# A quad's sums over states in another order, and the steps around a selective scan moved by one tick

## The chip, the core and the metric

The kernel runs on one core of a Trainium2 chip. Five instruction streams work side by side: TensorE (PE in the profile; its weight loads are PEld), VectorE (DVE), ScalarE (ACT), GpSimd (POOL) and SyncE (SP), which here issues nearly all DMAs. Each stream takes its instructions in the order in which the program holds them, and they meet through semaphores. The metric is the device time of one run in microseconds (us): 1186.88 us is the median of three runs of the kernel before (1186.69 to 1189.98).

## The reference

The input is x, 4 sequences of 1024 tokens with 256 features, all in float32. One layer is computed, in two parts:

```
h   = layernorm(x);  u = rmsnorm(h) * norm1_w
z, xs, B, C, dt_raw = split(u @ in_proj_w.T)        # 256, 64, 64, 256, 128 columns
dt  = softplus(dt_raw @ dt_proj_w.T + b)
state = exp(dt * A) * state + (dt * xs) * B          # per channel and state, along 1024 tokens
y   = (sum over states of state * C + xs * D) * silu(z)
h   = h + y @ out_proj_w.T
x   = x + h + (silu(n @ gate.T) * (n @ up.T)) @ down.T    # n = rmsnorm(h) * norm2_w, width 704
x   = x + (fwht(silu(v @ W1.T) * (v @ W3.T))) @ W2.T      # v = layernorm(x), width 1024
```

There are 256 channels with 32 states each: 8192 recurrences for each sequence. The Walsh-Hadamard transform (fwht) is worked into W2 once, at the start.

## The kernel before

**Units and quads.** The tokens are cut into eight units of 512 (two for each sequence, `us`). The recurrences of a unit are cut into 16 quads (`qs`, 128 in all); a quad holds four tiles (b = 0 to 3) of 128 partitions (32 states x 4 channels) by 512 tokens. The second unit of each sequence (units 1, 3, 5, 7, called odd here) starts its states from the `carry` of the first; the even ones start from a constant.

**Ticks.** The order of all instructions is written out by hand, by a loop over ticks at the end of `tile_block`. A quad takes two ticks, a half of it (two tiles) each; a unit takes 32 ticks. In tick T, for the quad q = T // 2, the loop emits, stream by stream:

- PE: the steps of lane `PE`, then (in even ticks) `sum_states(q - 1)`, then lane `PEend`
- ACT: lane `ACT`, then `copy_b` where there is one, two `exp` for the quad after this one (they are what the scans of tick T + 2 read), then lane `ACTend`
- DVE: `times_b` for the two tiles, a scan, the steps of lane `DVE`, the other scan
- POOL: lane `POOL0`, `times_c` for the two tiles scanned in tick T - 1, `start_from` (odd units: the first column of the tiles of tick T + 1 times the carry), then lane `POOL`
- SP: DMA issues: `ub` for tick T + 6, `da` for three quads on, `cr` for two quads on

The four steps of a tile are `da = exp(dt * A)` (ACT, L725), `bx = ub * B` (DVE, L749, two tiles in one), the scan (DVE, L759) and the product with C (POOL, L777, two tiles in one). `sum_states` (L791) then sums over states with four matmuls against a 0/1 matrix, one for each tile, into four groups of 32 output partitions. Each of these float32 matmuls appears twice in the profile. A `da` tile has four buffers, and one is loaded again when the sums have read it. B stands in PSUM as `pb`, one buffer, copied by `copy_b` (L738) every 16 ticks, between the last `times_b` that reads the old one and the first that reads the new one.

**The steps around the scan.** `pre(u, H)` prepares unit u, whose first tick is H, during the ticks of the unit before: normalization (`un`, transposed to `ut`), the projections of x, B and dt (`pe_x`), dt (`pe_dt`), C (`pe_c`) and z (`pe_z`). `post(u, E, other)` does what follows the scan of unit u, whose last tick is E, during the ticks of the next unit, here with ticks counted from E:

- E+3: out_proj, 8 matmuls on PE (`add_rows` with `wo`, L306); two DVE adds at E+4 (L316)
- E+5 to E+9: row statistics, 1/sqrt (`small2`, POOL), scaling (`hn`, ACT), transposes to `ht`
- E+10 and E+13: `gated` on `m`, three chunks each: gate and up projections (PE, L226), `silus` and the copies `up` (ACT, L263 and L270), products (POOL, L274); the z of the unit after next rides along as a further projection
- E+18: down projection (`add_rows` with `wd`), statistics, `hn`, transposes to `xt` at E+25
- E+26, E+29, E+32: `gated` on `g` in chunks of 3, 3 and 2; E+36: `add_rows` with `w2h`; E+43: store

So E+32 is tick E of the next unit: while out_proj of unit u runs, the last chunk of `g` of the unit before and then its `w2h` matmuls run too. The steps of `pre` for the unit after next fall in the same ticks: with H = E + 33, H-30 is E+3, H-25 is E+8, H-16 is E+17.

The lines that matter in `gated`, for a group that starts at `tick`:

```
for k, step in enumerate(steps):
    at(tick + k // 2, "PE", *step)          # gate projections, z, up projections
at(tick + 1, "ACTend" if three else "ACT", silus)
at(tick + 2, "ACT", up, 0)                  # the others: ACTend of tick + 2
at(tick + 2, "POOL", product, 0)            # the others: tick + 3
```

PSUM has four buffers for all dense results (`ps_m`); `ht`, `xt`, `ut` and `yt` share three buffers, `un` and `hn` share one.

Of the kernel before, what the change touches and what calls it, by code (L numbers as in the profile page):

```python
# [11 lines left out]
ALU = mybir.AluOpType  # L12
# [8 lines left out]
TT = T // P  # L21
# [6 lines left out]
def tile_block(ctx: ExitStack, tc: tile.TileContext, a, out):  # L28
# [20 lines left out]
    nc = tc.nc  # L49
# [15 lines left out]
    def dense_psum():  # L65
        return ps_m.tile([P, T], F32, tag="dense", name="dense")
# [141 lines left out]
    def transposes(u, src):  # L208

        u["pt"] = [dense_psum() for _ in range(2)]  # L210
        for k in range(2):
            for t in range(TT):
                nc.tensor.transpose(  # L213
                    u["pt"][k][:, t * P : (t + 1) * P], src[:, t, k * P : (k + 1) * P], ident
                )
# [22 lines left out]
    def at(tick, lane, fn, *args):  # L238
        todo[tick][lane].append(partial(fn, *args))
# [5 lines left out]
    def gated(tick, u, dst, wa, wb, chunks, src, z=None):  # L245


        g = [{} for _ in chunks]
        pe_z, act_z = z[0]["z"] if z else (None, None)

        def pe(i, name, w):
            c, n = chunks[i]
            if n < P:

                both = project(W[w], c * P, 2 * n, u[src])
                g[i]["pg"], g[i]["pu"] = both, both[n:]
            else:
                g[i][name] = project(W[w], c * P, n, u[src])

        def silus():  # L260
            for i, (_, n) in enumerate(chunks):
                g[i]["si"] = p3.tile([P, T], F32, tag="si", name="si")
                nc.scalar.activation(g[i]["si"][:n], g[i]["pg"][:n], AF.Silu)  # L263
            if z:
                act_z(z[1])

        def up(i):
            n = chunks[i][1]
            g[i]["up"] = p3.tile([P, T], F32, tag="up", name="up")
            nc.scalar.copy(g[i]["up"][:n], g[i]["pu"][:n])  # L270

        def product(i):
            c, n = chunks[i]
            nc.gpsimd.tensor_tensor(u[dst][:n, c, :], g[i]["si"][:n], g[i]["up"][:n], ALU.mult)  # L274

        three = len(chunks) == 3
        steps = [(i, *s) for s in (("pg", wa), ("pu", wb)) for i in range(len(chunks))]
        steps = [s for s in steps if chunks[s[0]][1] == P or s[1] == "pg"]
        late = z and len(steps) == 6
        steps = [(pe, *s) for s in steps]  # L280
        if z:
            steps.insert(3, (pe_z, z[1]))
        for k, step in enumerate(steps):
            at(tick + k // 2, "PE", *step)
        at(tick + 1, "ACTend" if three else "ACT", silus)
        at(tick + 2, "ACT", up, 0)
        for i in range(1, len(chunks)):
            if i == 2 and late:
                at(tick + 3, "ACT", up, i)
            else:  # L290
                at(tick + 2, "ACTend", up, i)
        at(tick + 2, "POOL", product, 0)
        for i in range(1, len(chunks)):
            at(tick + 3, "POOL", product, i)
# [29 lines left out]
    def pre(u, H):  # L324

        s = {}
# [217 lines left out]
        if H == 32:  # L544

            at(0, "ACTend", lambda: row_stats(u, u["x"], (0, 1)))
            at(1, "ACTend", lambda: row_stats(u, u["x"], (2, 3)))
            at(3, "POOL", small)
            at(5, "POOL", small_end)
            at(4, "ACT", un, (0, 1))  # L550
            at(5, "ACT", un, (2, 3))
            at(6, "PE", lambda: transposes(u, s["un"]))
            at(6, "ACTend", transposed, u, "ut")
        else:
            at(H - 54, "SP", load_x, u)
            at(H - 45, "ACTend", lambda: row_stats(u, u["x"], (0, 1)))
            at(H - 43, "ACTend", lambda: row_stats(u, u["x"], (2, 3)))
            at(H - 39, "POOL", small)
            at(H - 37, "POOL", small_end)
            at(H - 32, "ACT", un, (0, 1))  # L560
            at(H - 31, "ACT", un, (2, 3))
            at(H - 30, "PE", lambda: transposes(u, s["un"]))
            at(H - 30, "ACTend", transposed, u, "ut")
        at(H - 25, "PE", pe_x)
        at(H - 24, "ACT", act_x)
        at(H - 23, "SP", dma_xb)
        at(H - 19, "SPend", dma_xr, 0)
        at(H - 17, "SPend", dma_xr, 1)
        at(H - 16, "PE", pe_dt)
        at(H - 16, "PE", pe_c, 0)  # L570
        if H == 32:
            for h in range(2):
                at(H - 11, "PE", pe_z, h)
# [16 lines left out]
    def post(u, E, other):  # L590


        s = {}
# [41 lines left out]
            4,  # L635
            "PEend",
        )
        at(E + 5, "ACTend", lambda: row_stats(u, u["hr"], (0, 1), False))
        at(E + 6, "ACTend", lambda: row_stats(u, u["hr"], (2, 3), False))
        at(E + 7, "POOL", small2)  # L640
        at(E + 8, "ACT", hn, "r3", None)
        at(E + 9, "PE", lambda: transposes(u, s["tok"]))
        at(E + 9, "ACTend", transposed, u, "ht")
        at(E + 9, "POOL", lambda: nc.gpsimd.tensor_tensor(u["hr"], u["hr"], u["x"], ALU.add))
        at(E + 10, "PE", big, "m")
        sizes = [min(P, DFF - c * P) for c in range(6)]
        chunks = list(enumerate(sizes))
        for i in range(2):
            gated(E + 10 + 3 * i, u, "m", "wg", "wu", chunks[3 * i : 3 * i + 3], "ht",
                  (other, i) if other else None)  # L650
        add_rows(
            E + 18,
            u,
            lambda: [u["m"][:n, c, :] for c, n in enumerate(sizes)],
            lambda: [W["wd"][:n, c, :] for c, n in enumerate(sizes)],
            1,
        )
        at(E + 20, "ACTend", lambda: row_stats(u, u["hr"], (0, 1)))
        at(E + 22, "ACTend", lambda: row_stats(u, u["hr"], (2, 3)))
        at(E + 23, "POOL", small3)  # L660
        at(E + 24, "ACT", hn, "r4", "nm")
        at(E + 25, "PE", lambda: transposes(u, s["tok"]))
        at(E + 25, "ACTend", transposed, u, "xt")
        at(E + 26, "PE", big, "g")
        chunks8 = [(c, P) for c in range(8)]
        for i in range(3):
            gated(E + 26 + 3 * i, u, "g", "w1", "w3", chunks8[3 * i : 3 * i + 3], "xt")
        add_rows(
            E + 36,
            u,  # L670
# [113 lines left out]
    def sum_states(q):  # L784
        s = qs[q]
        u = s["u"]
        first, last = s["n"] % 8 == 0, s["n"] % 8 == 7
        if first:
            u["py"] = ps_y.tile([P, T], F32, tag="y", name="py")
        for b in range(4):  # L790
            nc.tensor.matmul(  # L791
                u["py"][32 * b : 32 * b + 32, :],
                lhsT=rsel[:, 2 * s["j"] + s["g"], :],
                rhs=s["da"][:, b, :],
                start=first,
                stop=last,
            )
        if last:
            at(2 * q + 3, "DVE", y_dx, u, s["h"])
            at(2 * q + 4, "POOL0", y_z, u, s["h"])  # L800
# [13 lines left out]
    for k, u in enumerate(us):  # L814
        pre(u, 32 * k)
# [37 lines left out]
    tick = min(todo)  # L853
# [106 lines left out]
```

## Time and profile before

| what | value |
|---|---|
| time, median of 3 runs | 1186.88 us (1186.69 to 1189.98) |
| the profiled execution's own time | 1190.86 us |
| its span (first to last instruction) | 1189.1 us |
| mean granted TensorE clock | 0.903 |
| DVE busy | 961.1 us (81%) |
| PE busy | 1023.6 us (86%) |
| POOL busy | 903.0 us (76%) |
| ACT busy | 773.8 us (65%) |
| first scan starts, last scan ends | 22.2 us, 1074.0 us |

How to read it: groups of instructions are named by line, engine and operation, output <- inputs; then how often, busy us and mean ns of one, and, behind the second bar, the idle time of the engine right before them and what ended it. A wait is "engine, line of what waited <- engine, line of what it waited for: us in total, times, longest". A row of the timeline is start us, us, engine, line, operation, output <- inputs, number of merged instructions; in square brackets is the idle time before it with its releaser. A row of windows is a stretch (from:to, length) and then the busy us of PE, PEld, DVE, ACT and POOL, each with its number of instructions, the granted PE clock, the busy share of the DMA engines and GB/s. The rows of one period quoted later are of unit 3 (fourth of eight), where E is tick 95 and tick 96 begins its scans at 419.17 us.

### The profile page before, as it was taken

The numbers are of one execution on the slowest core, as the hardware profiler recorded it, in microseconds if no ns is written. First come the engines' busy times: TensorE is split into PE (matmuls) and PEld (weight loads), VectorE is DVE, ScalarE is ACT, GpSimd is POOL, SyncE is SP. The second block draws the span as 40 slices with busy tenths as digits, with TensorE's granted clock in tenths as the row PEclk, the third lists the DMA queues.
The fourth block names the chain that finished last, engine by engine and source line by source line (L and its number), as shares of the span: only waits on it lengthen the run. The fifth ranks groups of instructions, "written<-read, shape, count | busy, mean of one in ns | idle before, by whom it ended". The sixth has DMA issues, their size and how long they took to land.

```text
span 1189.1 us, 12244 instructions
## 1 busy us (share of the span) xinstructions
PE 1023.6 (86%) x3374; PEld 471.1 (40%) x3374; DVE 961.1 (81%) x860; ACT 773.8 (65%) x1391; POOL 903.0 (76%) x807
## 2 busy tenths in 40 slices
PE   8475467989998989988998989988998989699988
PEld 3121022433633355433634354433634353336535
DVE  4797889899889979899889979898989989992000
ACT  3746564878478775879478767878576847573331
POOL 6675768879788978889788978889787978784212
PEclk9776668989898889989998989988998989889989
DMA  7989998898699879888799869998689869840000
GB/s 246 336 308 355 358 338 296 310 329 284 238 337 306 327 244 313 318 327 296 252 339 313 302 225 342 313 335 282 242 315 322 308 243 328 307 155 1 18 0 18
DMA packets 89444, 321.91 MB, mean 271 GB/s; under 512 B 9312, under 2 KB 20000, under 8 KB 73120
## 3 DMA queue, kind: packets, MB, share of 16 engines
q1 hardware_dynamic: 87520, 318.38, 75.7%
q10 hardware_dynamic: 1856, 2.75, 0.6%
q8 instruction: 27, 0.44, 0.1%
q14 instruction: 41, 0.34, 0.1%
HBM read 302.22 MB, written 18.87 MB: 270 GB/s over the span
## 4 chain that ended last, share of the span: by engine, by line
PE 44%; POOL 16%; DVE 10%; issue 8%; DMA 4%; ACT 4%; SPq 0%; DVEq 0%; POOLq 0%; ACTq 0%
PE dense L226 23%; PE dense L306 14%; POOL da L777 10%; PE py L791 6%; DVE da L759 5%; DVE bx L749 4%; POOL g L274 3%; ACT da L725 1%; DMA ub<-ud 1%; DMA cd<-cc 1%; POOL m L274 1%; DVE hr L316 1%; PE dense L213 1%; DMA xr<-xbd 1%; POOL yt L811 1%
## 5 line engine op out<-in xcount | busy, mean ns | idle before, releaser
L777 POOL TENSOR_TENSOR da<-da,cr 128x1024 f32<-128x1024 f32 x256 | 603.7, 2358 | 100.1 <-DVE da L759 52.2
L759 DVE TENSOR_TENSOR_SCAN da<-da,bx 128x512 f32<-128x512 f32 x512 | 602.0, 1210 | 43.7 <-ACT da L725 10.4
L725 ACT ACTIVATE da<-da,nega 128x512 f32<-128x512 f32 x508 | 331.4, 713 | 68.8 <-DMA da<-dtd 65.4
L791 PE MATMUL py<-da,rsel 128*32 128x512 f32 x1024 | 226.7, 685 | 134.7 <-POOL da L777 132.8
L749 DVE TENSOR_TENSOR bx<-ub,pb 128x1024 f32<-128x1024 f32 x254 | 312.1, 1229 | 30.5 <-ACT pb L738 19.2
L226 PE MATMUL dense<-xt,w 128*128 128x512 f32 x512 | 228.8, 601 | 0.0
L226 PEld LDWEIGHTS dense<-xt,w 128*128 128x128 f32 x512 | 95.6, 191 | 136.0 <-issue 111.8
L791 PEld LDWEIGHTS py<-da,rsel 128*32 128x32 f32 x1024 | 29.9, 113 | 270.7 <-POOL da L777 213.8
L316 DVE TENSOR_TENSOR hr<-hr,dense 128x512 f32<-128x512 f32 x48 | 32.4, 675 | 127.6 <-PE dense L306 127.6
L306 PE MATMUL dense<-w2h,g 128*128 128x256 f32 x512 | 113.4, 380 | 0.0
L306 PE MATMUL dense<-wd,m 128*128 128x256 f32 (+1 forms) x384 | 103.6, 417 | 0.9 <-POOL m L274 0.9
L306 PEld LDWEIGHTS dense<-w2h,g 128*128 128x128 f32 x512 | 96.8, 190 | 18.4 <-issue 5.5
L270 ACT COPY up<-dense 128x512 f32<-128x512 f32 x112 | 63.4, 578 | 58.3 <-PE dense L226 58.1
L274 POOL TENSOR_TENSOR g<-si,up 128x512 f32<-128x512 f32 x64 | 80.8, 1272 | 25.8 <-ACT up L270 25.4
L226 PE MATMUL dense<-ut,win 128*128 128x512 f32 x192 | 94.1, 623 | 0.2 <-ACT ut L220 0.2
L274 POOL TENSOR_TENSOR m<-si,up 128x512 f32<-128x512 f32 (+1 forms) x48 | 60.4, 1273 | 41.3 <-ACT up L270 41.3
L226 PE MATMUL dense<-ht,wg 128*128 128x512 f32 x192 | 89.4, 610 | 2.6 <-ACT ht L220 2.6
L263 ACT ACTIVATE si<-dense 128x512 f32<-128x512 f32 x112 | 63.0, 596 | 39.7 <-PE dense L226 38.1
L306 PEld LDWEIGHTS dense<-wd,m 128*128 128x128 f32 (+1 forms) x384 | 72.3, 201 | 40.0 <-issue 24.0
L200 ACT ACTIVATE hn<-hr,s 128x256 f32<-128x256 f32 x64 | 30.3, 543 | 88.9 <-POOL s L196 74.8
L226 PE MATMUL dense<-ht,wu 128*128 128x512 f32 x160 | 72.2, 597 | 0.0
L776 POOL COPY carry<-da 128x2 f32<-128x2 f32 x128 | 23.8, 186 | 61.5 <-DVE da L759 59.5
(92 smaller groups left out, 798.5 us busy)
## 6 DMA issues: line engine op xcount, KB each, us to landing
da<-dtd SPq DMA_DIRECT2D x127, 1024.0 KB
ub<-ud SPq DMA_DIRECT2D x254, 512.0 KB
cr<-cd SPq DMA_DIRECT2D x64, 256.0 KB
x<-in_x SPq DMA_DIRECT2D x8, 512.0 KB
dtd<-dt SPq DMA_DIRECT2D x16, 256.0 KB
ud<-du SPq DMA_DIRECT2D x16, 256.0 KB
cd<-cc SPq DMA_DIRECT2D x16, 256.0 KB
out<-hr SPq DMA_DIRECT2D x8, 512.0 KB
```

The source lines that it names most:

```text
L200: nc.scalar.activation(dst[:, t, :], src[:, t, :], AF.Identity, bias=bias[:, t : t + 1] if bias is not None else 0.0, scale=scale[:, t : t ...
L226: nc.tensor.matmul(dst[:n], lhsT=w[:, k, col : col + n], rhs=src[:, k, :], start=(k == 0), stop=(k == 1),)
L263: nc.scalar.activation(g[i]["si"][:n], g[i]["pg"][:n], AF.Silu)
L270: nc.scalar.copy(g[i]["up"][:n], g[i]["pu"][:n])
L274: nc.gpsimd.tensor_tensor(u[dst][:n, c, :], g[i]["si"][:n], g[i]["up"][:n], ALU.mult)
L306: nc.tensor.matmul(po[t // 2][:, t % 2, :], lhsT=left[k][:, t * P : (t + 1) * P], rhs=right[k], start=(k == 0), stop=(k == n - 1),)
L316: nc.vector.tensor_tensor(hr, hr, po[i], ALU.add)
L725: nc.scalar.activation(da, da if q else s["u"]["pdt", b], AF.Exp, scale=an[:, s["h"], s["j"], b, s["g"] : s["g"] + 1],)
L749: nc.vector.tensor_tensor(s["bx"], s["ub", b0 // 2], u["pb"].unsqueeze(1).broadcast_to([P, 2, T]), ALU.mult)
L759: nc.vector.tensor_tensor_scan(da, da, s["bx"][:, b % 2, :], start, ALU.mult, ALU.add)
L777: nc.gpsimd.tensor_tensor(s["da"][:, two, :], s["da"][:, two, :], s["cr"].unsqueeze(1).broadcast_to([P, 2, T]), ALU.mult,)
L791: nc.tensor.matmul(u["py"][32 * b : 32 * b + 32, :], lhsT=rsel[:, 2 * s["j"] + s["g"], :], rhs=s["da"][:, b, :], start=first, stop=last,)
```

## The change

`sum_states` multiplies the tiles in the order 2, 3, 0, 1 instead of 0, 1, 2, 3. Nearly all steps of `post` from the row statistics after out_proj to the last gated group are emitted one tick earlier, as are `un`, its transposes, `pe_dt` and the first `pe_c` of `pre`; both halves of the first row statistics stand in one tick. out_proj itself, its adds, `pe_x`, `act_dt`, `copy_b`, and the `w2h` matmuls keep their ticks. `silus` of the group of two chunks goes to the end of its tick on ACT. The first unit's and the second unit's preparation keep most of their ticks.

```diff
-        three = len(chunks) == 3
...
-        at(tick + 1, "ACTend" if three else "ACT", silus)
+        at(tick + 1, "ACTend", silus)
...
-            at(H - 32, "ACT", un, (0, 1))
-            at(H - 31, "ACT", un, (2, 3))
-            at(H - 30, "PE", lambda: transposes(u, s["un"]))
-            at(H - 30, "ACTend", transposed, u, "ut")
-        at(H - 25, "PE", pe_x)
-        at(H - 24, "ACT", act_x)
-        at(H - 23, "SP", dma_xb)
+            at(H - 33, "ACT", un, (0, 1))
+            at(H - 32, "ACT", un, (2, 3))
+            at(H - 31, "PE", lambda: transposes(u, s["un"]))
+            at(H - 31, "ACTend", transposed, u, "ut")
+        x = max(H - 25, 7)
+        at(x, "PE", pe_x)
+        at(x + 1, "ACT", act_x)
+        at(x + 2, "SP", dma_xb)
...
-        at(H - 16, "PE", pe_dt)
-        at(H - 16, "PE", pe_c, 0)
+        at(H - 17, "PE", pe_dt)
+        at(H - 17, "PE", pe_c, 0)
...
-        at(E + 5, "ACTend", lambda: row_stats(u, u["hr"], (0, 1), False))
-        at(E + 6, "ACTend", lambda: row_stats(u, u["hr"], (2, 3), False))
-        at(E + 7, "POOL", small2)
-        at(E + 8, "ACT", hn, "r3", None)
-        at(E + 9, "PE", lambda: transposes(u, s["tok"]))
-        at(E + 9, "ACTend", transposed, u, "ht")
-        at(E + 9, "POOL", lambda: nc.gpsimd.tensor_tensor(u["hr"], u["hr"], u["x"], ALU.add))
-        at(E + 10, "PE", big, "m")
+        at(E + 5, "ACTend", lambda: row_stats(u, u["hr"], range(TT), False))
+        at(E + 6, "POOL", small2)
+        at(E + 7, "ACT", hn, "r3", None)
+        at(E + 8, "PE", lambda: transposes(u, s["tok"]))
+        at(E + 8, "ACTend", transposed, u, "ht")
+        at(E + 8, "POOL", lambda: nc.gpsimd.tensor_tensor(u["hr"], u["hr"], u["x"], ALU.add))
+        at(E + 9, "PE", big, "m")
...
-            gated(E + 10 + 3 * i, u, "m", "wg", "wu", chunks[3 * i : 3 * i + 3], "ht",
+            gated(E + 9 + 3 * i, u, "m", "wg", "wu", chunks[3 * i : 3 * i + 3], "ht",
...
         add_rows(
-            E + 18,
+            E + 17,
...
-        at(E + 20, "ACTend", lambda: row_stats(u, u["hr"], (0, 1)))
-        at(E + 22, "ACTend", lambda: row_stats(u, u["hr"], (2, 3)))
-        at(E + 23, "POOL", small3)
-        at(E + 24, "ACT", hn, "r4", "nm")
-        at(E + 25, "PE", lambda: transposes(u, s["tok"]))
-        at(E + 25, "ACTend", transposed, u, "xt")
-        at(E + 26, "PE", big, "g")
+        at(E + 19, "ACTend", lambda: row_stats(u, u["hr"], (0, 1)))
+        at(E + 21, "ACTend", lambda: row_stats(u, u["hr"], (2, 3)))
+        at(E + 22, "POOL", small3)
+        at(E + 23, "ACT", hn, "r4", "nm")
+        at(E + 24, "PE", lambda: transposes(u, s["tok"]))
+        at(E + 24, "ACTend", transposed, u, "xt")
+        at(E + 25, "PE", big, "g")
...
-            gated(E + 26 + 3 * i, u, "g", "w1", "w3", chunks8[3 * i : 3 * i + 3], "xt")
+            gated(E + 25 + 3 * i, u, "g", "w1", "w3", chunks8[3 * i : 3 * i + 3], "xt")
...
-        for b in range(4):
+
+        for b in (2, 3, 0, 1):
```

## The prediction

> **What bounds the kernel now.** I read the page first (busy shares, costliest groups), then the waits, then the timeline of each engine over unit 3.
>
> ```profile
> PE 1023.6 (86%) x3374; PEld 471.1 (40%) x3374; DVE 961.1 (81%) x860; ACT 773.8 (65%) x1391; POOL 903.0 (76%) x807
> L777 POOL TENSOR_TENSOR da<-da,cr 128x1024 f32<-128x1024 f32 x256 | 603.7, 2358 | 100.1 <-DVE da L759 52.2
> L759 DVE TENSOR_TENSOR_SCAN da<-da,bx 128x512 f32<-128x512 f32 x512 | 602.0, 1210 | 43.7 <-ACT da L725 10.4
> L749 DVE TENSOR_TENSOR bx<-ub,pb 128x1024 f32<-128x1024 f32 x254 | 312.1, 1229 | 30.5 <-ACT pb L738 19.2
> ```
>
> A tick on DVE is two scans and one product: 2.33 + 1.23 us and gaps, 3.70 from one tick's first scan to the next, the floor. 256 ticks make 947 us of the 1052 between first and last scan. The other 105 are the added DVE work (adds, yt) and stalls. The stalls have names:
>
> ```profile
> DVE hr L316 <- PE dense L306: 127.6, 22, 43.3
> DVE bx L749 <- ACT pb L738: 19.2, 8, 3.7
> ```
>
> Part of the first is in the tail. Taking scan starts tick by tick, E+4 (out_proj's adds) takes 8.6 to 10.2 us in units 1 to 7 instead of 3.70 + 2 x 0.59 = 4.88: 31 us together. E+16 (copy of B) takes 6.1 to 6.3 in units 1 to 6: 15 us. Nearly every other tick is at its floor. So 46 us is the most that letting out_proj and the copies "stand alone" can win. What the E+16 stall hangs on:
>
> ```profile
> 440.00:487.00 47.00, 46.77 (x177) 24.03 (x176) 44.82 (x39) 27.58 (x47) 37.95 (x31) 1.00 0.82 290
> ...
> 484.32 0.58 ACT L270 COPY up<-dense 128x512 f32<-128x512 f32 x1 [1.18 <-PE dense L226]
> 484.93 1.28 ACT L725 ACT_TABLE_LOAD   x1
> 486.22 1.33 ACT L725 ACTIVATE da<-da,nega 128x512 f32<-128x512 f32 x2
> 487.46 1.17 ACT L270 COPY up<-dense 128x512 f32<-128x512 f32 x2
> 488.53 0.58 ACT L738 COPY pb<-br 128x512 f32<-128x512 f32 x1
> ...
> 482.64 0.20 POOL L766 TENSOR_TENSOR da<-da,carry 128x2 f32<-128x2 f32 x1
> 484.99 1.27 POOL L274 TENSOR_TENSOR m<-si,up 128x512 f32<-128x512 f32 x1 [2.15 <-ACT up L270]
> 486.21 2.37 POOL L777 TENSOR_TENSOR da<-da,cr 128x1024 f32<-128x1024 f32 x1
> 488.53 0.20 POOL L766 TENSOR_TENSOR da<-da,carry 128x2 f32<-128x2 f32 x1
> ...
> 484.40 2.33 DVE L759 TENSOR_TENSOR_SCAN da<-da,bx 128x512 f32<-128x512 f32 x2
> 489.15 1.23 DVE L749 TENSOR_TENSOR bx<-ub,pb 128x1024 f32<-128x1024 f32 x1 [2.41 <-ACT pb L738]
> ```
>
> PE is busy 46.77 of 47 us: from out_proj (433.43) to the last up projection of `m` (485.95) it works without a break through w2h, x, `m`. `up` waits for PE; exps, copies and POOL's product queue behind it. This stretch is bound by PE, whatever tick its steps are written in.
>
> **Part 1, the second group of `m` (E+13 to E+12).** PE's list between out_proj and the last up holds the same matmuls. Two things move inside. The sums of tick E+9 (459.40, 1.35 us) fill PE's wait for `ht` (459.47 to 460.98); now two gate projections go first, so PE waits there and the sums come on top, 1.0 us. ACT copies `ht` before x and dt, but the gate needs PSUM that x's copy frees: start 460.85. Net: the first up projection ends 0.8 us later, 485.0 instead of 484.2. But `up` now stands ahead of the exps of tick 109, not 110, and these feed scan 111, which starts at 484.40 now.
> - Even unit: up 485.7, table load 487.0, exps 488.3 (scan 111 late by 3.3), two ups 489.4, the exps of tick 110 490.8, copy of B 491.4, product 492.6, scan 112 at 492.7 instead of 490.47: **+2.2 us** in units 2, 4, 6.
> - Odd unit: POOL's product waits for `up` too, ahead of times_c and of the carry step (L766) that scan 111 waits for: 485.7 + 1.27 + 2.37 + 0.2 = scan 111 at 489.65; then two products (2.5), times_c, carry step: scan 112 at 494.75: **+4.3 us** in units 3 and 5. Stalls from the first group (scan 108, up to 2 us) lie inside this sum, as the end hangs on PE.
> - Unit 1: PE has no w2h and idles before x, but `small2` now sits in E+6 behind `du` (1.27 + 1.5 us), pushing times_c and the sums that precede x on PE by 1.4; the same chain then gives +5.4. Unit 7 lacks x and z: +0.5.
>
> Together 3 x 2.2 + 2 x 4.3 + 5.4 + 0.5 = 21.1 us. Bounds: -2.5 in each of six units (the whole stall goes) to +5.4 in each.
>
> **Part 2, `g` one tick earlier, up to out_proj.** Out_proj follows, on PE, sums that wait for POOL:
>
> ```profile
> 426.72 1.28 POOL L274 TENSOR_TENSOR g<-si,up 128x512 f32<-128x512 f32 x1
> 427.96 1.26 POOL L811 TENSOR_TENSOR yt<-yt,zs 128x512 f32<-128x512 f32 x1
> 429.19 2.34 POOL L777 TENSOR_TENSOR da<-da,cr 128x1024 f32<-128x1024 f32 x1
> ...
> 426.68 1.05 PE L791 MATMUL py<-da,rsel 128*32 128x512 f32 x4 [0.39 <-POOL da L777]
> 431.58 1.92 PE L791 MATMUL py<-da,rsel 128*32 128x512 f32 x4 [3.85 <-POOL da L777]
> ```
>
> The transposes of `un` that leave E+3 ran at 425.19, before any of this: moving them frees nothing. One `g` product still precedes yt on POOL: the first product is gone from that place, the second has come. POOL's load per tick is 2.36 + 0.2 plus extras against 3.70, so it recovers about 1.0 us per tick. Today `small_end` (1.9 with gaps) and one product (1.27) share E+28 and two products E+29; now `small_end` and two products (2.5) share E+28. The backlog there grows from 2.2-2.5 to 4.7-5.0 us, beyond the 2.4 at which the carry step holds a scan. Carried through by the same rows: odd to even (three times) +1.0 at E+30 and +0.2 at out_proj; even to odd (twice) scan 96 at 421.9 instead of 419.17, part regained because the 1.57 us stall before scan 97 goes: +1.75; into unit 7 +1.5. Together 8.6 us; bounds 0 (backlog absorbed) to 14 (2 each).
>
> **Part 3, the order of the sums.** Tiles 0 and 1 ran while PE waited for 2 and 3; now all four run behind that wait, side by side. Four tiles together took 1.06 to 1.47 us (423.80: 1.47), two 1.05, so the path gets 0 to 0.4 longer per unit at full clock, twice that at half; below nothing only if four packed tiles end sooner than two, which no row shows. I take 0.15 x 7 = 1.
> The clock: in the fence, two tiles took 1.92 behind an idle 3.85 us against 1.05, and the granted clock was 0.5 from 430.3 to 437.1. The Trainium skill (TensorE: Matmul & The Clock Gate, "HAM oscillation") says that an idle window of about 3.4 us halves the clock, and so speaks against an edit that merges PE's idle times; by it one more cold window per out_proj (3.4 us at half speed) would add 7 x 1.7 = 12 us. The row says the clock is already low when out_proj starts; I add none.
>
> **At nothing.** dt and C at E+16, the down projection, statistics and `xt` a tick earlier lie in E+17 to E+24, where PE was busy 31.02 of 38 us (487 to 525) and no tick is over its floor but for adds; without that cover, 1 us each. The tail behind the last scan (115 us) has no exps and one order of dependences: `silus` moved on ACT is worth at most a table load (1.28) either way. SP: x's copy lands 3.8 us later (456.92 to 460.7), four ticks before its reader; the sums of E+9, E+11 and E+13 end about 5 us later, so the `da` loads behind them on SP, and the `ub` loads behind those, start later; exps there end 6 to 16 us ahead of their scans, which covers it. Uncovered: up to 5 us a unit.
>
> **Sum.** 21.1 + 8.6 + 1 = 30.7, against the profiled execution 1190.86: 1221.6. That execution is 4 us above the median, so 1218 in terms of the median.
>
> **The rivals.**
> 1. *The gated groups really start a tick earlier* (the other side). Then `up` is done before copy_b's tick and the E+16 stalls go: 6 x 2.5 = 15 us, 1172; with part of out_proj's 31 us, 1160. It decides where the first up projection ends 3.2 us earlier (by 481.0 in unit 3, so that two exps are ready at 484.40). For it: PE waits 0.3 + 0.23 us around the `ht` transposes, and POOL's `small2` leaves E+7. Against: 46.77 of 47 us busy.
> 2. *ACT and POOL absorb most of it*: PE's end stays where it is and backlogs dissolve as at E+10 today (1.2 to 0.14 us). Only exps of two ticks in front of copy_b count: 6 x 1.4, and part 2 at a third, 3: 1198.
> 3. *No change*: every moved step ends when PE lets it and the reordered waits cancel: 1187.
> 4. *Loads run late*: the 5 us shift of the sums reaches the exps in units 2 to 6, 5 x 4 on top: 1238.
>
> **How the numbers follow.** Forecast 0.50 (its own range 1205 to 1230), rival 1 0.20, rival 2 0.17, rival 3 0.05, rival 4 0.08. About 0.3% (3.6 us) is what can be told from no change. Slower: 0.50 + 0.17 + 0.08; faster 0.20; same 0.05. Range 1178 to 1238: it leaves out most of rival 1 and what lies beyond rival 4.
>
> **What the profile after would show.** Part 1: ticks E+15 and E+16 both over 3.70, DVE's scan waiting for ACT da or POOL L766, the wait for L738 no longer alone; PE still full from out_proj to the last up. Part 2: longer waits of scans for L766 at E+30 and around E+32, E+4 ticks still 8.6 to 10.5. Part 3: the sums as x8 behind the wait for POOL. I am wrong if the E+16 ticks fall to 3.70 with E+15 at 3.70, or if PE shows gaps between out_proj and the last up that let it end sooner.

## The result and the profile after

The changed kernel takes 1215.32 us (median of 4 runs, 1213.36 to 1217.32), against 1187.64 us (4 runs, 1186.69 to 1189.98) of the kernel before, run beside it: a ratio of 1.023, with a 95% interval of 1.0207 to 1.0253. It is slower. The profiled execution took 1215.46 us (span 1213.7). Its first scan starts at 22.6 us and its last ends at 1100.8 us, 26.4 us more between the two than before; the tail behind the last scan is 112.9 us, 2.2 less.

From the page of the kernel after, the busy shares and the groups that answer to those shown of before (most lines of the code have moved up by one):

```profile
PE 972.6 (80%) x3374; PEld 465.3 (38%) x3374; DVE 960.8 (79%) x860; ACT 778.4 (64%) x1393; POOL 902.1 (74%) x807
L776 POOL TENSOR_TENSOR da<-da,cr 128x1024 f32<-128x1024 f32 x256 | 603.3, 2357 | 94.5 <-DVE da L758 46.5
L758 DVE TENSOR_TENSOR_SCAN da<-da,bx 128x512 f32<-128x512 f32 x512 | 601.8, 1209 | 72.8 <-POOL da L765 30.8
L748 DVE TENSOR_TENSOR bx<-ub,pb 128x1024 f32<-128x1024 f32 x254 | 312.2, 1229 | 18.7 <-ACT pb L737 7.6
```

DVE does the same work in the same time. What grew is its idle time ahead of the scans, 43.7 to 72.8 us, and the largest part of it, 30.8 us, now ends with POOL's carry step (L765). The waits of the kernel after, for DVE, say the same:

```profile
DVE hr L315 <- PE dense L305: 126.6, 22, 43.4
DVE da L758 <- POOL da L765: 30.8, 17, 3.3
DVE da L758 <- ACT da L724: 16.4, 9, 2.6
DVE yt L806 <- PE py L791: 15.6, 4, 4.6
DVE bx L748 <- ACT pb L737: 7.6, 7, 3.2
```

The wait of the product for the copy of B fell from 19.2 to 7.6 us, so in this narrow sense the copies do stand more alone. In its place came longer waits of scans for POOL and for exps (10.4 us before) and of `yt` for the sums. The rows of before for the first and the last of these:

```profile
DVE yt L806 <- PE py L791: 7.2, 2, 7.0
DVE da L759 <- POOL da L766: 6.3, 6, 1.6
```

The longest wait of `yt` lies in the tail in both kernels (7.0 us before, 4.6 after), so what is new inside the scans is some 11 us. The wait for out_proj (127.6 before) is what it was.

From one tick's first scan to the next, summed over the eight units and set against the profile of before (us):

| ticks | after minus before | where |
|---|---|---|
| E+1 to E+3 | -3.6 | E+1 of units 3 and 5 at its floor |
| E+4 | -1.5 | adds of out_proj |
| E+5 to E+11 | +0.2 | |
| E+12 to E+17 | +14.1 | 5.1 in unit 1, 3.5 and 3.1 in units 3 and 5, 1.0 in units 2, 4, 6 |
| E+18 | +10.4 | 3.4 to 3.7 in units 2, 4, 6, nowhere else |
| E+19 to E+27 | -1.0 | unit 0 |
| E+28 to E+32 | +7.7 | E+29 of units 1, 3 and 5 1.9, E+30 of them -0.9; E+32 of units 2 and 4 2.2 |
| all | +26.4 | |

What happens in E+12 to E+16 of unit 3 is seen in DVE's timeline after, from the scans of tick 108 to those of tick 112:

```profile
483.04 2.33 DVE L758 TENSOR_TENSOR_SCAN da<-da,bx 128x512 f32<-128x512 f32 x2 [1.35 <-POOL da L765]
...
487.95 2.33 DVE L758 TENSOR_TENSOR_SCAN da<-da,bx 128x512 f32<-128x512 f32 x2 [1.32 <-POOL da L765]
...
497.49 2.33 DVE L758 TENSOR_TENSOR_SCAN da<-da,bx 128x512 f32<-128x512 f32 x2 [2.25 <-POOL da L765]
499.91 1.23 DVE L748 TENSOR_TENSOR bx<-ub,pb 128x1024 f32<-128x1024 f32 x1
502.41 1.22 DVE L758 TENSOR_TENSOR_SCAN da<-da,bx 128x512 f32<-128x512 f32 x1 [1.27 <-POOL da L765]
```

and in POOL's, in the same stretch:

```profile
493.73 1.26 POOL L274 TENSOR_TENSOR m<-si,up 128x512 f32<-128x512 f32 x1 [3.34 <-ACT up L270]
494.95 2.35 POOL L776 TENSOR_TENSOR da<-da,cr 128x1024 f32<-128x1024 f32 x1
497.26 0.20 POOL L765 TENSOR_TENSOR da<-da,carry 128x2 f32<-128x2 f32 x1
497.40 2.51 POOL L274 TENSOR_TENSOR m<-si,up 128x512 f32<-128x512 f32 x2
```

POOL takes its instructions in order. The product of the second group waits 3.34 us for `up`; behind it stand the product with C and the carry step, and for that the scan at 497.49 waits. The product for the new B (499.91) waits for nothing.

Even units have no carry step; there the exps stand behind `up`. ACT and DVE in the tick E+15 of unit 4:

```profile
628.63 0.58 ACT L270 COPY up<-dense 128x512 f32<-128x512 f32 x1 [2.37 <-PE dense L226]
...
631.29 2.33 DVE L758 TENSOR_TENSOR_SCAN da<-da,bx 128x512 f32<-128x512 f32 x2 [2.56 <-ACT da L724]
```

The first gate of unit 3 starts right behind the first copy of `ht`, ahead of x's copy. PE and ACT:

```profile
468.53 1.98 PE L226 MATMUL dense<-ht,wg 128*128 128x512 f32 x4 [0.24 <-ACT ht L220]
...
467.89 1.07 ACT L220 COPY ht<-dense 128x512 f32<-128x512 f32 x2 [5.05 <-PE dense L213]
468.85 0.60 ACT L367 COPY xb<-dense 128x512 f32<-128x512 f32 x1
```

### The profile page after: what moved, and what is told of

The parts are those of the page before. It is cut to its first block, busy times and chain, and to the rows that moved or that the text cites. A ratio compares the mean times of both kernels' runs of the same rounds, so it can differ in the third digit from the quotient of the medians.

```text
span 1213.7 us, 12192 instructions
## 1 busy us (share of the span) xinstructions
PE 972.6 (80%) x3374; PEld 465.3 (38%) x3374; DVE 960.8 (79%) x860; ACT 778.4 (64%) x1393; POOL 902.1 (74%) x807
## 5 line engine op out<-in xcount | busy, mean ns | idle before, releaser
L758 DVE TENSOR_TENSOR_SCAN da<-da,bx 128x512 f32<-128x512 f32 x512 | 601.8, 1209 | 72.8 <-POOL da L765 30.8
L724 ACT ACTIVATE da<-da,nega 128x512 f32<-128x512 f32 x508 | 332.0, 714 | 46.6 <-DMA da<-dtd 43.9
L791 PE MATMUL py<-da,rsel 128*32 128x512 f32 x1024 | 167.1, 731 | 218.0 <-POOL da L776 218.0
L226 PE MATMUL dense<-xt,w 128*128 128x512 f32 x512 | 233.8, 609 | 0.0
L791 PEld LDWEIGHTS py<-da,rsel 128*32 128x32 f32 x1024 | 21.4, 115 | 307.8 <-POOL da L776 275.5
L270 ACT COPY up<-dense 128x512 f32<-128x512 f32 x112 | 64.0, 579 | 73.0 <-PE dense L226 72.8
L226 PE MATMUL dense<-ut,win 128*128 128x512 f32 x192 | 105.1, 684 | 0.2 <-ACT ut L220 0.2
L305 PE MATMUL dense<-wd,m 128*128 128x256 f32 (+1 forms) x384 | 97.5, 397 | 0.9 <-POOL m L274 0.9
L305 PEld LDWEIGHTS dense<-wd,m 128*128 128x128 f32 (+1 forms) x384 | 68.8, 191 | 38.7 <-issue 28.9
```

Source lines behind the costliest of these rows:

```text
L226: nc.tensor.matmul(dst[:n], lhsT=w[:, k, col : col + n], rhs=src[:, k, :], start=(k == 0), stop=(k == 1),)
L305: nc.tensor.matmul(po[t // 2][:, t % 2, :], lhsT=left[k][:, t * P : (t + 1) * P], rhs=right[k], start=(k == 0), stop=(k == n - 1),)
L724: nc.scalar.activation(da, da if q else s["u"]["pdt", b], AF.Exp, scale=an[:, s["h"], s["j"], b, s["g"] : s["g"] + 1],)
L758: nc.vector.tensor_tensor_scan(da, da, s["bx"][:, b % 2, :], start, ALU.mult, ALU.add)
L791: nc.tensor.matmul(u["py"][32 * b : 32 * b + 32, :], lhsT=rsel[:, 2 * s["j"] + s["g"], :], rhs=s["da"][:, b, :], start=first, stop=last,)
```

## The experiments

Regions of every run, us against the profile of before, from one profiled execution each. A few us of this scatter from run to run, above all in unit 0. The column "E+28 to E+3" joins the end of one unit to the start of the next; "tail" is the time behind the last scan.

| kernel | time, us | E+12 to E+17 | E+18 | E+28 to E+3 | E+4 | tail |
|---|---|---|---|---|---|---|
| after | 1215.32 | +14.1 | +10.4 | +4.1 | -1.5 | -2.2 |
| after, old order of sums | 1209.25 | +16.6 | +2.0 | +4.5 | +1.1 | -2.3 |
| before, new order of sums | 1197.84 | -0.7 | +0.1 | +7.3 | -2.6 | +3.2 |
| after, second group of m back | 1203.76 | +11.5 | -0.6 | +4.9 | -0.5 | -1.7 |
| after, whole chain of m back | 1193.13 | +1.4 | -0.2 | +4.5 | -0.9 | -1.6 |
| after, wd behind the sums | 1217.34 | +14.0 | +2.2 | +4.4 | +0.2 | -1.7 |
| after, wd to g back | 1210.81 | +14.8 | +2.0 | +9.1 | -6.1 | +3.0 |
| after, wd to g and un back | 1210.21 | +14.3 | +2.0 | +6.8 | -5.2 | +3.0 |
| before, light | 1171.07 | -1.5 | -0.2 | -0.9 | -1.7 | -13.9 |
| after, light | 1199.01 | +18.5 | +2.1 | +4.3 | -0.2 | -16.6 |
| before, second group of m later | 1179.26 | -7.1 | 0.0 | -0.5 | -4.4 | +0.4 |
| the same, up behind the copy of B | 1171.29 | -15.2 | 0.0 | +2.4 | -1.8 | +0.7 |
| the same, adds of out_proj later | 1169.65 | -12.4 | +2.4 | +4.1 | -39.4 | +0.6 |

Two rows have a large entry outside these columns: with wd behind the sums E+19 to E+27 is 7.7 us longer, and with the adds later E+5 to E+11 is 26.4 us longer.

### The order of the sums

In the changed kernel:

```diff
-        for b in (2, 3, 0, 1):
+        for b in range(4):
```

> The changed kernel with the sums over states in the old order 0, 1, 2, 3. Theory: the order is worth 0 to 0.4 us a unit, so the run lies within 3 us of the changed kernel (1212 to 1217), and the stalls from E+12 to E+18 (24.5 us over the kernel before, by scan starts) and from E+28 to E+32 (7.7 us) stand. Rival: the order makes the sums run late behind each merged wait and so sets the E+18 stall; then the run is 5 us or more below the changed kernel.

Measured: 1209.25 us (1207.97 to 1210.76), 6.1 below the changed kernel. The rival was right. The gain is in E+18 of units 2, 4 and 6, which went from 8.1 to 5.3 us, and 2.6 us of it are lost again at E+4. PE's timeline in unit 4 shows how. In the kernel after:

```profile
633.17 1.93 PE L791 MATMUL py<-da,rsel 128*32 128x512 f32 x8 [2.91 <-POOL da L776]
635.04 3.78 PE L391 MATMUL dense<-raw,dtw 128*128 128x512 f32 x4
638.61 2.21 PE L226 MATMUL dense<-ut,win 128*128 128x512 f32 x4
640.66 2.95 PE L305 MATMUL dense<-wd,m 128*128 128x256 f32 x12
643.54 1.06 PE L791 MATMUL py<-da,rsel 128*32 128x512 f32 x8
```

and with the old order:

```profile
629.87 1.05 PE L791 MATMUL py<-da,rsel 128*32 128x512 f32 x4
632.86 1.05 PE L791 MATMUL py<-da,rsel 128*32 128x512 f32 x4 [1.94 <-POOL da L776]
633.84 1.98 PE L391 MATMUL dense<-raw,dtw 128*128 128x512 f32 x4
635.66 1.88 PE L226 MATMUL dense<-ut,win 128*128 128x512 f32 x4
637.38 2.95 PE L305 MATMUL dense<-wd,m 128*128 128x256 f32 x12
```

With the old order the first two tiles cut the wait: 1.94 us of idle time instead of 2.91. Behind it PE ran at full speed (granted clock 1.00 from 632.86 to 637.38); behind the 2.91 us it did not (0.59 from 633.17 to 640.66), and dt took 3.78 us instead of 1.98. PE then lies further behind, and `yt`, which needs the sums of 643.54, held DVE for 3.63 us:

```profile
644.67 0.75 DVE L806 SCALAR_TENSOR_TENSOR yt<-xr,dpar,py 128x512 f32<-128x512 f32 x1 [3.63 <-PE py L791]
```

That is nearly what the Trainium skill (TensorE: Matmul & The Clock Gate, "HAM oscillation") describes, an idle window that halves the clock; its 3.4 us is longer than the 2.91 us that sufficed here.

The other direction, on the kernel before:

```diff
-        for b in range(4):
+        for b in (2, 3, 0, 1):
```

> The kernel before with only the order of the sums changed to 2, 3, 0, 1. Theory, after the run of the changed kernel with the old order (8.4 us won back at E+18 of units 2, 4 and 6, where two tiles now shorten PE's idle time from 2.91 to 1.94 us and dt took 1.99 instead of 3.78 us; 2.5 us lost at E+4): the new order costs only where a wait of nearly 3 us or more comes before work that PE cannot hide. Before has no wait of that length ahead of E+16, so only E+4 changes, by 0 to -3 us in total: 1184 to 1189. Rival, the rule on the clock as the prediction weighed it (one more slow window per out_proj): 12 us more, 1199.

Measured: 1197.84 us (1196.95 to 1199.4), a ratio of 1.0072 (1.0052 to 1.0093), 9.5 us more. The theory missed: E+4 did get 2.6 us shorter, but E+28 to E+3 lost 7.3 and the tail 3.2. The rival had the size and not the place, since out_proj is where the new order gains. The loss is in `g`. PE's timeline ahead of the last group of `g` in the last unit, with the new order:

```profile
1049.77 1.94 PE L791 MATMUL py<-da,rsel 128*32 128x512 f32 x8 [1.75 <-POOL da L777]
1051.63 8.98 PE L226 MATMUL dense<-xt,w 128*128 128x512 f32 x16
```

and before:

```profile
1045.12 3.44 PE L791 MATMUL py<-da,rsel 128*32 128x512 f32 x8
1048.49 7.13 PE L226 MATMUL dense<-xt,w 128*128 128x512 f32 x16
```

In before two tiles run inside the wait (the row of 3.44 us holds both pairs), and the sixteen rows of projections behind them take 7.13 us. With the new order PE is idle for those 1.75 us, and the same sixteen take 8.98 (granted clock 0.74 from 1049.77 to 1060.54). In both runs PE was slow before this wait began: the transposes ahead of it took 2.81 us (1.04 ahead of the gates), and the granted clock was 0.50 from 1037.9 to 1048.1 in before and from 1041.7 to 1055.4 with the new order. So here the early tiles did not keep the clock up, they brought it back sooner. It is the same in every unit: the first sixteen rows of `g` take 8.2 to 9.0 us with the new order and 7.1 to 7.4 in before. From there to the end of `g` PE has no gap in which to win this back.

### The chain of m

The second group back at E+13, in the changed kernel:

```diff
-            gated(E + 9 + 3 * i, u, "m", "wg", "wu", chunks[3 * i : 3 * i + 3], "ht",
+            gated(E + 9 + 4 * i, u, "m", "wg", "wu", chunks[3 * i : 3 * i + 3], "ht",
```

> The changed kernel with the second group of m back at E+13. Theory: the second group in front of the copy of B makes the excess of 24.5 us in E+12 to E+18, so most of it goes and the time falls by 18 to 24 us, to 1191 to 1197; the waits of scans for POOL's carry step shrink, and the stall at E+16 alone is back at about 2.5 us. Rival: the excess comes from the first group, from small2 and from wd, each a tick earlier; then the time falls by less than 8 us.

Measured: 1203.76 us (1202.15 to 1205.75), 11.6 below the changed kernel, between the two expectations. Of the 24.5 us in E+12 to E+18, 13.5 go: all of E+18, and E+15 is back at its floor in every unit. What stays are stalls of 1.25 us at both E+12 and E+13 of units 3 and 5 (together 4.1 in unit 1), which are the first group's, and 7.4 to 7.7 us at E+16 of even units.

The whole chain back:

```diff
-        at(E + 5, "ACTend", lambda: row_stats(u, u["hr"], range(TT), False))
-        at(E + 6, "POOL", small2)
...
-            gated(E + 9 + 3 * i, u, "m", "wg", "wu", chunks[3 * i : 3 * i + 3], "ht",
+        at(E + 5, "ACTend", lambda: row_stats(u, u["hr"], (0, 1), False))
+        at(E + 6, "ACTend", lambda: row_stats(u, u["hr"], (2, 3), False))
+        at(E + 7, "POOL", small2)
...
+            gated(E + 10 + 3 * i, u, "m", "wg", "wu", chunks[3 * i : 3 * i + 3], "ht",
```

> The changed kernel with the whole chain of m back at its old ticks: statistics, small2, hn, transposes to ht, both groups. Putting back the second group alone took 13.5 of the 24.5 us of E+12 to E+18 away. Theory: the rest (stalls at E+12 and E+13 of odd units, 2.5 us each, 4.1 in unit 1, and 1.4 at E+16 of even units) is the first group's, so E+12 to E+18 comes to within 4 us of before, and the time to 1192 to 1197. Rival: the rest is made by x, dt and C and by wd, which stay early; then the time stays above 1200.

Measured: 1193.13 us (1192.04 to 1194.35), as the theory had it: 22.2 us of the 27.7 are the chain of `m`. E+12 to E+18 is 1.2 us over before, although x, dt, C, wd and the new order stay.

The last pair, called light, asks whether PE is what binds this stretch. It leaves out half of the `w2h` product, in both kernels:

```diff
-            lambda: [u["g"][:, c, :] for c in range(8)],
-            lambda: [w2h[:, c, :] for c in range(8)],
+            lambda: [u["g"][:, c, :] for c in range(4)],
+            lambda: [w2h[:, c, :] for c in range(4)],
```

> The kernel before with half of the last matrix product left out (4 of 8 chunks of w2h, at E+4 to E+7), so PE has 7 us less to do in each unit ahead of m. Theory: the stretch from out_proj to the last up is bound by PE, so the tick E+16 falls from 6.2 to below 4.3 us in units 1 to 6, 12 us, and the tail loses 7 to 14 us: 1161 to 1170. Rival: the copy of B waits for ACT's own queue; then E+16 stays at 6 us and only the tail gains, 1174 to 1181.

> The changed kernel with the same half of the last matrix product left out. Theory: with PE ahead, the groups of m really end a tick earlier and E+12 to E+18 is within 6 us of the light kernel before it, instead of 24.5 us over: the light pair differs by less than 10 us, against 27 us for the full pair. Rival: the cost lies in the order on ACT and POOL alone, whatever PE has to do: the light pair differs by 20 us or more.

Measured: 1171.07 us (1170.14 to 1171.7) and 1199.01 us (1196.72 to 1199.44). They differ by 27.9 us, the full pair by 27.7. The second rival was right, and the first in its mechanism: E+16 of the light kernel before still takes 5.8 us in units 2 to 6, and two thirds of what its profile gains lies in the tail, though its time is below that rival's range. With 7 us less to do in each unit, PE starts the gates hardly earlier or not at all: in unit 3 the first gate comes 2.4 us behind the first scan of E+9 in before and 2.1 in its light form, 1.5 after and 2.3 in its light form. The other units from 2 to 6 agree: 0.3 to 0.7 us earlier in before, 0.7 to 1.0 later in the changed kernel. Windows of the kernel after, from out_proj's sums to the first gate and from there to the last up (busy time of PE is the second number of each row):

```profile
441.59:468.53 26.94, 26.70 (x121) 18.41 (x121) 22.36 (x22) 9.50 (x23) 19.59 (x16) 0.94 0.59 231
468.53:494.69 26.16, 26.16 (x76) 10.01 (x76) 22.87 (x20) 19.17 (x29) 17.32 (x16) 1.00 0.87 311
```

and of the light one:

```profile
441.99:468.67 26.68, 21.38 (x85) 13.43 (x81) 21.42 (x20) 8.05 (x20) 17.88 (x16) 0.82 0.70 234
468.67:494.83 26.16, 26.16 (x76) 10.03 (x76) 22.11 (x20) 19.16 (x29) 17.15 (x14) 1.00 0.83 295
```

PE's timeline of the light kernel shows what it waits for:

```profile
452.65 3.72 PE L305 MATMUL dense<-w2h,g 128*128 128x256 f32 x16
460.42 1.93 PE L791 MATMUL py<-da,rsel 128*32 128x512 f32 x8 [4.05 <-POOL da L776]
462.28 5.28 PE L226 MATMUL dense<-ut,win 128*128 128x512 f32 x8
467.39 1.04 PE L213 MATMUL dense<-ident,hn 128*128 128x128 f32 x8
```

On PE the gates stand behind the transposes of `hn`, these behind x, and x behind the sums emitted in E+7, which wait for POOL's product with C. `hn` was done at 459.8, 7.6 us before its transposes began. Less work did let PE take these sums earlier: 6.0 us ahead of the first scan of E+9 (466.42) instead of 4.3 (462.72 and 467.02 in the full kernel). But behind 4.05 us of idle time the sums and x took 1.93 and 5.28 us instead of 1.06 and 3.70, which loses 2.4 us and so more than the 1.7 gained. In the light kernel before x ran at full speed (3.70 us), and there the first gate came behind sums of E+9 that had waited 1.30 us for POOL.

So in the kernel before, the first gate is held by its place in PE's order and by what the sums wait for, hardly by the amount of PE's work in front of it. For the changed kernel the pair shows less, since taking work away also slowed the clock (0.82 in the window instead of 0.94): at full speed the gate would have come some 1.7 us earlier, an estimate from the rows above, of the 5.3 us of work taken out. Only behind the first gate is PE really full: 24.97 of 24.97 us in before, 26.16 of 26.16 in the changed kernel, full and light.

### The down projection, g and un

Three edits of the changed kernel. First the down projection behind the sums of its tick:

```diff
             lambda: [W["wd"][:n, c, :] for c, n in enumerate(sizes)],
             1,
+            "PEend",
```

> The changed kernel with the down projection of E+17 in lane PEend, so that it stands behind the sums of that tick on PE. Theory: the 8.1 us tick E+18 of even units waits for sums that stand behind the first half of wd (2.95 us); with wd behind them it shrinks by 2 to 3 us in units 2, 4 and 6, so the time is 6 to 9 us below the changed kernel. Rival: the late up, POOL's late product and a PE at half speed after 2.9 us without work make the sums late by themselves, and only the place of dt and C ahead of them counts; then less than 3 us is won.

Measured: 1217.34 us (1216.87 to 1217.63), no gain. E+18 shrinks as the theory said, to 5.3 or 5.4 us in the even units (8.2 us in all), but the first add of wd, at E+19, now waits for wd. DVE's timeline in unit 4 has both waits:

```profile
644.17 0.75 DVE L807 SCALAR_TENSOR_TENSOR yt<-xr,dpar,py 128x512 f32<-128x512 f32 x1 [0.91 <-PE py L792]
...
650.10 0.69 DVE L315 TENSOR_TENSOR hr<-hr,dense 128x512 f32<-128x512 f32 x1 [1.48 <-PE dense L305]
```

Over all units E+19 to E+27 is 8.6 us longer than in the changed kernel. PE is that much behind, and DVE meets it at whichever result of PE it needs next.

Then wd, its statistics and `g` back at their old ticks:

```diff
-            E + 17,
+            E + 18,
...
-        at(E + 22, "POOL", small3)
-        at(E + 23, "ACT", hn, "r4", "nm")
...
-            gated(E + 25 + 3 * i, u, "g", "w1", "w3", chunks8[3 * i : 3 * i + 3], "xt")
+        at(E + 23, "POOL", small3)
+        at(E + 24, "ACT", hn, "r4", "nm")
...
+            gated(E + 26 + 3 * i, u, "g", "w1", "w3", chunks8[3 * i : 3 * i + 3], "xt")
```

> The changed kernel with wd, its statistics, small3, hn, the transposes to xt and g back at their old ticks. Theory: E+28 to E+32 lose their 7.7 us, while E+1 to E+4 get worse by up to 5.1 us (what they lost by the change), and wd no longer stands ahead of the sums that the 8.1 us tick E+18 of even units waits for, which gives back up to 3 x 3 us: together 3 to 12 us less than the changed kernel, 1203 to 1212. Rival (as forecast, part 2 costs 8.6 us in E+28 to E+4 and the E+18 stall has another cause): 8 to 9 us less, with E+18 still at 8 us in even units.

Measured: 1210.81 us (1210.55 to 1211.4), 4.5 less, inside the theory's range but by another sum. E+18 gives back 8.4 us and E+4 4.7; the tail takes 5.2, E+1 to E+3 4.9, and E+28 to E+32 stays 7.8 us over before, though E+29 and E+30 are back at their old lengths. The new loss is E+32, 5.0 us in nearly every unit instead of 3.74 or 3.80. ACT's timeline at the end of unit 2:

```profile
423.05 1.05 ACT L270 COPY up<-dense 128x512 f32<-128x512 f32 x2
423.99 1.10 ACT L200 ACTIVATE un<-x,s 128x256 f32<-128x256 f32 x2
424.99 0.59 ACT L737 COPY pb<-br 128x512 f32<-128x512 f32 x1
```

Two tiles of `un`, which the change emits a tick earlier, stand ahead of the copy of B. Undone too:

```diff
-            at(H - 33, "ACT", un, (0, 1))
-            at(H - 32, "ACT", un, (2, 3))
+            at(H - 32, "ACT", un, (0, 1))
+            at(H - 31, "ACT", un, (2, 3))
```

> The changed kernel with wd to g back at their old ticks and un with its transposes back too. With wd to g back alone, E+28 to E+32 kept their 7.8 us: the ticks E+30 and E+29 were as before, but E+32 took 5.0 us in each unit instead of 3.74. Theory: there two tiles of un, now emitted one tick earlier, stand on ACT ahead of the copy of B; with un back the tick E+32 falls to 3.8 us, 7 us in total, and the run lies at 1202 to 1205. Rival: the copies of the last chunk of g hold the copy of B, un is hidden, and the time stays at 1209 to 1212.

Measured: 1210.21 us (1208.53 to 1211.73). E+32 falls to 4.0 us as the theory had it, 6.2 us less from E+28 to E+32, and the time does not follow. E+1 to E+3 rises by 3.9 us: E+2 takes 5.97 us in units 2, 4 and 6, as it does in units 4 and 6 of the kernel before with the new order. There `yt` waits 1.5 us for the last sums of the unit, which stand on PE behind sixteen rows of `g` (7.13 us). The stall that `un` made only stood ahead of one that PE makes two ticks later.

### The opposite of the change

In the kernel before, the second group of `m` a tick later:

```diff
-            gated(E + 10 + 3 * i, u, "m", "wg", "wu", chunks[3 * i : 3 * i + 3], "ht",
+            gated(E + 10 + 4 * i, u, "m", "wg", "wu", chunks[3 * i : 3 * i + 3], "ht",
```

> The kernel before with the second group of m one tick LATER (E+14 instead of E+13), the opposite of the change. Theory: the end of PE's work stays where it is, but copy of B then stands behind one copy of up and not behind exps, a table load and three copies, so the tick E+16 of units 1 to 6 falls from 6.2 to about 4 us, 10 to 14 us in total: 1174 to 1178. Rival: whatever waits for up is only moved, the exps or POOL's product hold a scan at E+17 or E+18 instead, and the time stays within 4 us of 1188.

Measured: 1179.26 us (1177.19 to 1179.92), 0.9912 of before (0.9892 to 0.9932): faster than both kernels. E+16, 6.1 to 6.4 us in units 1 to 6 of before, takes 4.5 to 4.9; the theory's 4 us was a little too good, as one copy of `up` still stands ahead of the copy of B. E+4 was 4.4 us shorter too, which the edit gives no reason for and the next run shows only in part. That copy moved behind it:

```diff
-        at(tick + 2, "ACT", up, 0)
+        at(tick + 2, "ACTend" if dst == "m" and chunks[0][0] else "ACT", up, 0)
...
-        at(tick + 2, "POOL", product, 0)
+        at(tick + (3 if dst == "m" and chunks[0][0] else 2), "POOL", product, 0)
```

> The kernel before with the second group of m at E+14, and its first copy of up emitted behind the copy of B and the exps of E+16 instead of ahead of them, its product one tick later. Theory: with the copy of B behind nothing that waits for PE, the tick E+16, 4.5 to 4.9 us with the group later alone, falls to 3.8 us: 4 to 6 us below that run, 1173 to 1176. Rival: the copy of B was as early as the old B allows, and the later product holds the down projection or POOL's carry step; 1178 to 1183.

Measured: 1171.29 us (1169.74 to 1176.22), 0.9865 of before (0.9843 to 0.9887). E+16 is at its floor, 3.74 or 3.85 us in units 1 to 6, as the theory had it. E+16 of these units gives 6.1 us, as much as the theory hoped for. The medians differ by more, 8.0 us, but the runs here spread over 6.5 us, and the profiled one (1175.15) is only 3.8 us below that of the run before. ACT's timeline in unit 4, with the group later alone:

```profile
612.15 0.59 ACT L270 COPY up<-dense 128x512 f32<-128x512 f32 x1 [2.37 <-PE dense L226]
612.63 0.60 ACT L738 COPY pb<-br 128x512 f32<-128x512 f32 x1
```

and with that copy behind:

```profile
605.51 0.59 ACT L738 COPY pb<-br 128x512 f32<-128x512 f32 x1
606.11 1.28 ACT L725 ACT_TABLE_LOAD   x1
607.41 1.33 ACT L725 ACTIVATE da<-da,nega 128x512 f32<-128x512 f32 x2
608.65 0.56 ACT L270 COPY up<-dense 128x512 f32<-128x512 f32 x1
```

Last, the adds of out_proj a tick later as well, with both halves of the statistics at E+6:

```diff
-                at(tick + t // per_tick + 1, "DVE", add, t // 2)
+                at(tick + t // per_tick + (2 if per_tick == 4 else 1), "DVE", add, t // 2)
```

> The run before this one with out_proj's adds on DVE at E+5 instead of E+4 and both halves of the statistics at E+6. Theory: DVE's wait of 4 us at E+4 is covered by the scans of E+4, but m is bound by PE from out_proj on, so DVE meets it again at E+8 to E+18 and wins a part, 5 to 15 us: 1160 to 1170. Rival: all of it is met again, or the dense PSUM buffers, held a tick longer, delay w2h; 1172 or more.

Measured: 1169.65 us (1167.5 to 1171.2), 0.9841 of before (0.9824 to 0.9857), the best of all, though its runs overlap those of the one above. The rival is nearly right: E+4 falls to its floor in units 1 to 7, 39.4 us less, of which 8.3 are the adds themselves (7 x 2 x 0.59), moved to E+5. 26.4 come back at once, in E+5 (4.9 to 6.2 us) and in E+6 (up to 6.8 instead of 4.28), where now the first add of `w2h` waits for PE (2.43 us in unit 3), and 5.2 more than in the run above in E+12 to E+18. Most of the 31 us at E+4 is PE's delay, which DVE meets at the next result it needs.

## Why the prediction was right, and where it was not

The forecast was 1218 us, the time is 1215.3. The sum was 30.7 us on the profiled execution; the two profiled executions differ by 24.6.

- **Part 1** (21.1 us): E+12 to E+18 is 24.5 us longer, and putting the chain of `m` back removes 23.3 of them. For odd units the mechanism is the one written down, step by step: `up` ahead of POOL's product, ahead of the product with C and the carry step. For even units it is too, up to E+17: `up` ahead of a table load and the exps. Units 3 and 5 pay 3.5 and 3.1 us instead of 4.3; unit 1 5.1 instead of 5.4; unit 7 -0.5 (E+12 to E+18) instead of +0.5.
- The step "the first up projection ends 0.8 us later" was too much. Counted from the first scan of E+9, the last up ends 0.3 us later in unit 3 (27.7 against 27.4) and 0.2 earlier in unit 4 (27.6 against 27.8). The sums that come on top cost 1.2 us (26.16 for 24.97 from the first gate to the last up), near the 1.0 of the sum. What failed is "the gate needs PSUM that x's copy frees": in unit 3 after, the first gate starts at 468.53 and x's copy only at 468.85. So the first gate comes 0.9 us sooner against the scan in unit 3, where the sum had 0.1, and 1.4 in unit 4. With 0.3 later and 0.2 earlier in place of 0.8 the terms become 3.8 for odd and 1.2 for even units, close to the 3.1 to 3.5 and 1.0 of E+12 to E+17.
- For even units E+18 costs another 3.4 to 3.7, which was in no term: the wait of `yt` for the sums, from the half clock and the early wd together. Each of the two edits that take away one of them leaves about 0.6 to 0.9.
- **The bound was wrong in its first half.** "This stretch is bound by PE, whatever tick its steps are written in" read 46.77 busy of 47 us as a cause. The light pair shows that ahead of the first gate PE's work could be cut without an earlier gate worth the name: 4 us less in before (27.32 to 23.45) brought it 0.3 us forward in unit 3. In the changed kernel 5 us less (26.70 to 21.38) brought nothing, there also because of the clock, and the change's cost stayed 22 us in E+12 to E+18 (light after minus light before). The number survived because the part that the sum used, from the first gate to the last up, is truly full.
- **Part 2** (8.6 us): E+28 to E+4 costs 2.6 us. The odd to even step was sized right (0.93 in place of 1.0, three times). Even to odd was put at 1.75, and E+32 does lose 2.2 us, but 1.5 comes back at E+1, where the old stall before scan 97 went; the entry into unit 7 cost nothing instead of 1.5. The tail, put at nothing, gains: with `g` early it is 112.8 to 113.5 us in five kernels, against 118.1 and 118.1 with it back and the new order kept. Taking `wd` to `g` back won 4.5 us, yet in E+28 to E+4 and the tail it made 5.6 us of loss; its gain is E+18. The move of `un` ahead of the copy of B was overlooked; it costs a visible stall at E+32 where nothing else stalls there, and no time that the run without it shows.
- **Part 3** (1 us) failed by the step "0 to 0.4 per unit" and by adding none for the clock. The order alone costs 9.5 us on the kernel before and 6.1 us in the changed one. The four tiles behind the wait are indeed as quick as two (1.94 against 1.92 us), and out_proj gains 2.6 us; what was missed is the work of the two early tiles inside the wait, which kept the clock up for the work behind it (E+16) or brought it back sooner (`g`). The 12 us that the prediction worked out from the Trainium skill's rule were nearer in size, for other places than the one they were put at.
- **At nothing**: dt and C early, statistics and the `da` loads were rightly left at nothing; SP's wait for the sums grew by 49.6 us in the trace (394.7 to 444.3), yet DVE's waits for loads of `ub` are 3.0 us in all in both kernels and those of the exps for loads of `da` fell from 65.4 to 43.9, so rival 4 did not come. wd early was not free (E+18).
- **Rival 1** needed E+15 and E+16 at 3.70; they are 5.8 to 6.2 and 4.8 to 4.9 in units 1 to 6. **Rival 2** had 3 us for part 2, about what was measured, and too little for `m`. What rival 1 wished for, stalls at E+16 gone, came from moving the group the other way.

By regions, then: 3.4 us too little in E+12 to E+18, 7 too much in E+28 to E+4 (parts 2 and 3), 2.2 of the tail not foreseen. By cause, the chain of `m` without the new order costs 18.6 us there (the run with the old order) and the order 6, while `g`, `un` and the statistics come out near nothing. The total was close partly because these cancelled.

## What to carry to other kernels

In an order written out by hand, emitting a step earlier doesn't make it run earlier if what it reads is late; it puts its wait ahead of everything behind it on that engine's queue. Look for what stands behind a waiting instruction and move the waiting one back: here that won 1.4%, where the change lost 2.3%. And a busy share of 100% is no proof of a bound: take work off the engine and see whether the end moves, and look at its clock as you do, since an engine with less to do can run slower, as PE did in the light kernel (0.82 instead of 0.94).

## What the runs showed of the hardware

- Small work inside a wait of PE paid twice here, as it shortened the idle time and kept the clock up. In the profile after, 50 groups of sums of eight rows stand behind an idle time of PE of over 1 us (between 60 us and the last scan). Of the 34 behind 2.81 us or more, 33 took 1.58 to 1.94 us instead of 1.06, and one 1.32 (behind 3.90); of the 16 behind 1.08 to 2.67 us only 2 were slow (1.76 and 1.93). This is no fixed limit: in the kernel before with the new order, six took 1.5 us or less behind 2.96 to 4.05 us, and seven took 1.93 or 1.94 behind 1.74 to 1.97, with PE slow already.
- Half speed outlasted the sums: behind 2.91 us of idle time the sums and dt ran slow for 5.6 us together in the kernel after, and in the kernel before with the new order sixteen projections of `g` took 8.98 instead of 7.13 us.
- Four tiles side by side (eight rows) took as long as two: 1.06 against 1.05 us at full speed, 1.93 against 1.92 at half.
